# The last convolution of a four-layer network: other engines for its evictions, stores and loads

## The chip, the cores and the metric

The kernel runs on one core of a Trainium2 chip. The core has five engines that run side by side: TensorE (PE in the profile; its weight loads have a row of their own, PEld), VectorE (DVE), ScalarE (ACT), GpSimd (POOL) and SyncE (SP), the last of which does no arithmetic. SyncE, ScalarE and GpSimd can issue transfers between the chip's memory and SBUF; the profile shows the issuing as SPq, ACTq and POOLq. Matrix products land in PSUM, which has eight banks of 512 float32 columns on each of 128 partitions. The metric is the device time of one execution in microseconds; less is better.

## The reference

The input x is (8 images, 16 channels, 256, 256) in float32. Four layers follow each other, and each adds a convolution-like function of the group-normalised x to x: capsule routing, a spline convolution, patch attention, and last a 3x3 convolution. Only the last one matters here:

```
x = x + conv(_gn(x), L3_conv_weight)     # 16 -> 16 channels, 3x3
```

The reference writes this convolution with Fourier transforms, and the border wraps around: row -1 is row 255. The corner rows and columns of the transform's diagonal pick all nine taps. The group norm has eight groups of two channels each, over one image.

## The kernel before, in words

The four layers run one after another, each layer's result going through a scratch tensor in the chip's memory. `layer3` begins when the last rows of the third layer's result are on their way to the scratch tensors `x3_0` to `x3_7`, one for each image.

**Layout.** An image lies in SBUF as 128 partitions: eight row residues times sixteen channels. A partition holds 32 rows of 258 columns, the two edge columns wrapped, and a 33rd row for the wrap at the bottom. The weights `ws` contain the reciprocal deviation of the image's group norm and the identity that adds x itself; `weights` makes them for the next image with one VectorE instruction. What the mean contributes is a bias for each output row, `stat[b][1]`.

**Steps and pairs.** An image is four steps (`s` = 0 to 3), handled as two pairs: steps 0 and 1, then steps 2 and 3. Sixteen pairs make the stage. For a step, `products` is called twice, with `q` = 0 and 1; each call issues 48 products of a 32x32 weight block with 32x512 data, three column shifts times four banks `j` times four column blocks `c`. The profile shows each product as two records, so that one call is 96 records and a pair 384. The order in a pair, on TensorE, is q=0 of the first step, q=0 of the second, q=1 of the first, q=1 of the second.

**PSUM.** The products of a step go to a tile `p3` of four banks (named `p` in the profile). The pool has two of them, so that a pair fills all of PSUM, and the next pair's first step reuses the first tile, its second step the second tile. After q=0 of a step, ScalarE copies a few elements of it to `seen`; q=1 of that step waits for this.

**Eviction and stores.** `finish` (L1532 to L1547) takes a step from PSUM to the SBUF tile `y3` (named `y` in the profile, three buffers): ScalarE evicts the tile's first two banks and adds the bias, then VectorE the other two. Eight stores of 128 KB follow, four issued by SyncE and four by ScalarE itself; a store at the image's lower edge is split in two.

**Loads.** The first image is mostly in SBUF already (`first`); the rest of it (`x3r`, `x3e`) is loaded at the stage's start. `fetch` loads a whole image, in four pieces of 1032 KB and one small one, into one of three buffers, from SyncE. Images 1 and 2 are fetched at the start; image n+2 is fetched after the first pair of image n. SyncE issues these between its stores.

**Order.** Inside `tc.manual_schedule()` each engine runs its instructions in the order in which the code issues them. The last image's group norm isn't known when the stage starts; its steps (`todo`, from `stats3_steps`) are laid in after the first six pairs, each with a small product into a tile `p3` of the same pool, and VectorE or ScalarE work.

The waits between engines are made by the framework from the tiles that an instruction reads and writes.

Of the kernel before, what the change touches and what calls it, by code (L numbers as in the profile page):

```python
# [10 lines left out]
F32 = mybir.dt.float32  # L11
AF = mybir.ActivationFunctionType
ALU = mybir.AluOpType
AX = mybir.AxisListType
PSUM = bass.MemoryType.PSUM
DRAM = bass.MemoryType.DRAM

B, C, H, W = 8, 16, 256, 256
P = 128
WP = W + 2  # L20
# [258 lines left out]
class _Net:  # L279
# [1195 lines left out]
    def layer3(self, images=range(B)):  # L1475

        nc, tc = self.nc, self.tc
        with ExitStack() as st:
            io = st.enter_context(tc.tile_pool(name="l3_io", bufs=2))
            psum = st.enter_context(tc.tile_pool(name="l3_ps", bufs=2, space=PSUM))
            stat = dict.fromkeys(images, self.bc3)

            def bank():
                t = []

                def get():  # L1490
                    if not t:
                        t.append(psum.tile([P, 4, 512], F32, name="p3"))
                    return t[0][:, 0]

                return get

            def fetch(b):
                xs = io.tile([P, 33, WP], F32, name="x3s", bufs=3)
                self.fetch3(b, 0, 33, xs)
                return lambda k, g: xs[32 * k : 32 * k + 32, g : g + 2]  # L1500

            def weights(b):
                ws = io.tile([P, 3, 2, 32], F32, name="ws3")
                nc.vector.scalar_tensor_tensor(
                    ws.rearrange("p d t m -> p (d t m)"),
                    self.w3.rearrange("p d t m -> p (d t m)"),
                    stat[b][0][:, 1, b : b + 1],
                    self.k["ident3"],
                    ALU.mult,
                    ALU.add,  # L1510
                )
                return ws

            def products(s, q, ws, xs, ps):

                for dw in range(3):
                    for j in range(4):
                        k = (j + q) % 4
                        for c in range(4):
                            g = 8 * s + 2 * c + (j + q) // 4  # L1520
                            nc.tensor.matmul(  # L1521
                                ps[32 * c : 32 * c + 32, j].rearrange("p (g w) -> p g w", w=W),
                                ws[32 * k : 32 * k + 32, dw, q],
                                xs(k, g)[:, :, dw : dw + W],
                                start=q == 0 and dw == 0,
                                stop=q == 1 and dw == 2,
                                skip_group_check=True,
                            )

            def finish(b, s, ps):  # L1530

                y = io.tile([P, 2, 4, W], F32, name="y3", bufs=3)  # L1532
                bias = stat[b][1][:, b : b + 1]
                src = ps.rearrange("p j (g w) -> p g j w", w=W)
                nc.scalar.activation(y[:, :, 0:2], src[:, :, 0:2], AF.Identity, bias=bias)
                nc.vector.tensor_scalar(y[:, :, 2:4], src[:, :, 2:4], bias, None, ALU.add)
                for c in range(4):
                    for ro in range(2):
                        row = 64 * s + 16 * c + 1 + ro
                        n = 8 if row + 14 < H else 7  # L1540
                        yc = y[32 * c : 32 * c + 32].rearrange("(o r) g j w -> r o (g j) w", r=2)[ro]
                        for first, m, at in ((0, n, row),) if n == 8 else ((0, 7, row), (7, 1, 0)):
                            to = self.out[b, 0, at]
                            (nc.scalar if c % 2 else nc.sync).dma_start(
                                out=bass.AP(tensor=to.tensor, offset=to.offset, ap=[[H * W, C], [2 * W, m], [1, W]]),
                                in_=yc[:, first : first + m],
                            )  # L1547

            images = list(images)
            rest = io.tile([P, 9, WP], F32, name="x3r", bufs=1)  # L1550
            self.fetch3(images[0], 24, 9, rest)
            edge = io.tile([P, 3, WP], F32, name="x3e", bufs=1)
            nc.sync.dma_start(
                out=edge, in_=self.x3[images[0]].rearrange("r c h k w -> (r c) (h k) w")[:, 23:26]
            )

            def first(k, g):
                part = slice(32 * k, 32 * k + 32)
                if g + 2 <= 24:
                    return self.x3s[part, g : g + 2]  # L1560
                return edge[part, g - 23 : g - 21] if g == 23 else rest[part, g - 24 : g - 22]

            seen = io.tile([P, 4], F32, name="seen", bufs=1)
            xs = {images[0]: first}
            ws = weights(images[0])

            stat[images[-1]], todo = self.stats3_steps(self.small, "g3b", bank)
            with tc.manual_schedule():
                for b in images[1:3]:
                    xs[b] = fetch(b)  # L1570
                for n, b in enumerate(images):
                    for s in (0, 2):
                        ps = [psum.tile([P, 4, 512], F32, name="p3") for _ in range(2)]
                        for q in range(2):
                            for k in range(2):
                                products(s + k, q, ws, xs[b], ps[k])
                                if q:
                                    finish(b, s + k, ps[k])
                                else:
                                    nc.scalar.copy(seen, ps[k][:, :, 0])  # L1580
                        if todo:
                            todo.pop(0)[2]()
                        while todo and todo[0][0] != "PE":
                            todo.pop(0)[2]()
                        if s == 0 and n + 1 < len(images):
                            if n and n + 2 < len(images):
                                xs[images[n + 2]] = fetch(images[n + 2])
                            ws_after = weights(images[n + 1])
                    if n + 1 < len(images):
                        ws = ws_after  # L1590
# [69 lines left out]
```

## Time and profile before

| What | us |
|---|---|
| Median of three runs (6789.7 to 6796.36) | 6793.12 |
| The profiled execution's own time | 6794.16 |
| Its span in the profile | 6792.4 |
| First product of the last convolution (from the span's start) | 6452.8 |
| End of its last product | 6779.2 |
| VectorE evictions, 128x1024, each | 1.284 |
| ScalarE evictions, 128x1024, each | 1.113 |

The profile's times count from the start of the span. A line of the timeline gives the start, the duration, the engine, the source line, the operation, output and inputs, and in square brackets how long the engine had been idle and what ended that. In the view of waits, a line names who waited, for whom, the total in microseconds, how often, and the longest. In the table of stretches, each engine has its busy time and number of instructions, and then come the granted TensorE clock (1.00 is full speed), the busy share of the 16 DMA engines, and GB/s. Line numbers are those of the code above: L1521 a product, L1535 ScalarE's eviction, L1536 VectorE's, L1544 a store, L1469 and L1473 an image's load, L1504 the weights, L1580 the copy to `seen`.

### The profile page before, as it was taken

The numbers are of one execution on the slowest core, as the hardware profiler recorded it, in microseconds if no ns is written. First come the engines' busy times: TensorE is split into PE (matmuls) and PEld (weight loads), VectorE is DVE, ScalarE is ACT, GpSimd is POOL, SyncE is SP. The second block draws the span as 40 slices with busy tenths as digits, with TensorE's granted clock in tenths as the row PEclk, the third lists the DMA queues.
The fourth block names the chain that finished last, engine by engine and source line by source line (L and its number), as shares of the span: only waits on it lengthen the run. The fifth ranks groups of instructions, "written<-read, shape, count | busy, mean of one in ns | idle before, by whom it ended". The sixth has DMA issues, their size and how long they took to land. (4 is left out here: it accounts for less than half of the span.)

```text
span 6792.4 us, 111546 instructions
## 1 busy us (share of the span) xinstructions
PE 6136.1 (90%) x46024; PEld 2773.5 (41%) x46024; DVE 5395.3 (79%) x6342; ACT 2738.6 (40%) x3898; POOL 3219.0 (47%) x2077
## 2 busy tenths in 40 slices
PE   3899889899898999899886999999999999999977
PEld 1333333333333333333332444444444566666643
DVE  5799999999999999999997999999999433333311
ACT  1333333333333333333331888888888222112211
POOL 0566666666666666666666344444443211111100
PEclk9999999999999999999997999999999999999988
DMA  6233333333333333333331555555556433433266
GB/s 257 60 89 92 95 87 93 92 89 87 87 87 87 87 92 95 91 89 93 92 88 57 188 175 176 175 175 175 176 177 182 136 80 95 102 92 81 61 205 182
DMA packets 394912, 801.07 MB, mean 118 GB/s; under 512 B 57506, under 2 KB 222626, under 8 KB 355106
## 3 DMA queue, kind: packets, MB, share of 16 engines
q1 hardware_dynamic: 342050, 743.33, 37.3%
q10 hardware_dynamic: 52352, 50.61, 2.5%
q8 instruction: 361, 5.91, 0.4%
q14 instruction: 149, 1.22, 0.1%
HBM read 583.07 MB, written 210.77 MB: 117 GB/s over the span
## 5 line engine op out<-in xcount | busy, mean ns | idle before, releaser
L745 POOL TENSOR_TENSOR dd<-dd 128x1024 f32<-128x1024 f32 x512 | 1213.8, 2371 | 616.8 <-DVE dd L736 596.7
L1001 PE MATMUL ps<-bases,tw 128*32 128x512 f32 (+1 forms) x13824 | 1361.3, 546 | 16.4 <-POOL bases L970 6.6
L736 DVE SCALAR_TENSOR_TENSOR dd<-rb,v 128x1024 f32<-128x1024 f32 (+1 forms) x1024 | 1066.9, 1083 | 96.8 <-PE rb L725 89.8
L970 POOL TENSOR_TENSOR bases<-e,a 128x1024 f32<-128x1024 f32 (+1 forms) x264 | 621.7, 2377 | 928.9 <-DVE e L968 928.6
L624 DVE TENSOR_TENSOR pr<-v,fb 128x2048 f32<-128x2048 f32 (+1 forms) x512 | 1011.5, 2017 | 24.3 <-PE pl L634 12.9
L518 PE MATMUL cv<-kt,w 128*128 128x512 f32 x2048 | 1001.3, 611 | 28.7 <-DVE dd L736 21.5
L527 ACT COPY v<-cv 128x1024 f32<-128x1024 f32 x512 | 517.1, 1010 | 1152.0 <-PE cv L522 1152.0
L1001 PEld LDWEIGHTS ps<-bases,tw 128*32 128x32 f32 x13824 | 597.3, 109 | 801.8 <-issue 483.8
L745 POOL TENSOR_TENSOR s<-s,dd 128x512 f32<-128x512 f32 x512 | 670.8, 1310 | 35.0
L725 PE MATMUL rb<-rs,ct_fold 32*128 32x512 f32 x3584 | 608.0, 648 | 71.3 <-ACT rs L707 67.9
L745 POOL TENSOR_TENSOR s<-v,dd 128x512 f32<-128x512 f32 x256 | 330.2, 1290 | 663.2 <-DVE dd L736 663.2
L634 PE MATMUL pl<-pr,ct_fold 128*32 128x512 f32 x3584 | 533.7, 608 | 120.7 <-DVE pr L624 120.7
L522 PE MATMUL cv<-kt,w 64*128 64x512 f32 x2048 | 578.3, 641 | 0.0
L518 PEld LDWEIGHTS cv<-kt,w 128*128 128x128 f32 x2048 | 354.9, 191 | 525.5 <-issue 300.5
L1415 PE MATMUL pqk<-w_qk,t 128*128 128x512 f32 x1024 | 484.2, 595 | 4.6 <-POOL t L1409 4.6
L1426 ACT ACTIVATE vt<-pv,w_b2v 128x128 f32<-128x128 f32 x512 | 146.2, 368 | 843.9 <-PE pv L1422 843.9
L1447 DVE TENSOR_TENSOR y<-po,res 128x512 f32<-128x512 f32 x128 | 88.5, 691 | 487.3 <-PE po L1442 487.3
L978 DVE SCALAR_TENSOR_TENSOR bases<-xr,xm,bases 128x1024 f32<-128x1024 f32 (+1 forms) x264 | 447.9, 1735 | 0.3 <-POOL bases L970 0.3
L1409 POOL TENSOR_TENSOR t<-t,emb 128x512 f32<-128x512 f32 x128 | 162.2, 1268 | 512.2 <-DVE t L1405 501.9
L955 ACT ACTIVATE sq<-a 128x1024 f32<-128x1024 f32 (+1 forms) x264 | 263.8, 999 | 230.0 <-DVE a L947 229.3
L725 PEld LDWEIGHTS rb<-rs,ct_fold 32*128 32x128 f32 x3584 | 172.8, 185 | 414.9 <-issue 219.3
L937 ACT ACTIVATE d<-xr,bd,sd 128x1024 f32<-128x1024 f32 (+1 forms) x264 | 319.1, 1209 | 15.7 <-DMA xr<-x1p 15.7
(260 smaller groups left out, 8386.8 us busy)
## 6 DMA issues: line engine op xcount, KB each, us to landing
kt<-d SPq DMA_DIRECT2D x256, 516.0 KB
xr<-x1p SPq DMA_DIRECT2D x120, 1024.0 KB
d<-dn ACTq DMA_DIRECT2D x64, 516.0 KB
x<-y SPq DMA_DIRECT2D x128, 258.0 KB
xs<-in_x_dram SPq DMA_DIRECT2D x16, 2048.0 KB
xs<-in_x_dram SPq DMA_DIRECT2D x64, 512.0 KB
res<-in_x_dram SPq DMA_DIRECT2D x64, 512.0 KB
x<-s SPq DMA_DIRECT2D x128, 256.0 KB
```

The costliest lines, as they stand in the source:

```text
L518: nc.tensor.matmul(ps()[:, n], w[:, 0, j, :], t[:, a : a + 2, 0:W], start=True, stop=False)
L522: nc.tensor.matmul(ps()[:, n], w[at, 1, j, :], t[at, a : a + 2, 2 - n : 2 - n + W], start=False, stop=True)
L527: nc.scalar.copy(v[h]()[:, 4 * g : 4 * g + 4, j * W : j * W + W], ps().rearrange("p n (a w) -> p (n a) w", w=W),)
L624: nc.vector.tensor_tensor(pr()[:, :n].rearrange("p n (r w) -> p n r w", w=W), v[h]()[:, 4 * g : 4 * g + n].rearrange("p n (r w) -> p n r w ...
L634: nc.tensor.matmul(pl()[at : at + 32], sel[:, g, h, :], pr()[:, t, :], start=h == 0 and g == 0, stop=h == 1 and (g == 1 or t == 3),)
L725: nc.tensor.matmul(r()[:, n], spread[at, g, h, :], rs()[at], start=True, stop=True)
L736: nc.vector.scalar_tensor_tensor(dd()[:, :n], r()[:, :n], 1.0 / B, v[h]()[:, a : a + n], ALU.subtract, ALU.mult)
L745: op("POOL", us, lambda: nc.gpsimd.tensor_tensor(out[0](), a[0](), b[0](), ALU.add), a[1] + b[1], out[1])
L970: nc.gpsimd.tensor_tensor(ring[n % 3][:, 0, p : p + m, 1 : 1 + W], rows(e), rows(a), ALU.subtract)
L978: nc.vector.scalar_tensor_tensor(r, rows(part[1]), xm[:, b : b + 1], v, ALU.is_gt, ALU.mult)
L1001: nc.tensor.matmul(out if k is None else out[:, k], lhs, rhs, start=start, stop=stop, skip_group_check=True)
L1415: nc.tensor.matmul(ps, t[:, n, k * P : (k + 1) * P], wqk[:, n, :], start=n == 0, stop=n == 1)
```

## The change

Four things change in `layer3`; the arithmetic stays.

- A step's PSUM tile of four banks becomes two tiles of two banks, from a pool of four. The small products of `todo` take one such tile.
- In `finish`, ScalarE evicts both halves of an even step, and VectorE both halves of an odd step. The copy to `seen` is divided in the same way, one for each half and with a tile of its own for each engine. `y3` has five buffers.
- SyncE issues all stores.
- GpSimd's queue loads half images of 17 or 16 rows (and the small wrapped piece), in one transfer each, into five buffers. Five halves are fetched at the start; from the fourth pair on, a pair begins by fetching the half that is needed four pairs later.

```
-            psum = st.enter_context(tc.tile_pool(name="l3_ps", bufs=2, space=PSUM))
+            psum = st.enter_context(tc.tile_pool(name="l3_ps", bufs=4, space=PSUM))
...
-            def fetch(b):
-                xs = io.tile([P, 33, WP], F32, name="x3s", bufs=3)
-                self.fetch3(b, 0, 33, xs)
-                return lambda k, g: xs[32 * k : 32 * k + 32, g : g + 2]
+            def fetch(n):
+                xs = io.tile([P, 17, WP], F32, name="x3s", bufs=5)
+                rows = self.x3[images[n // 2]].rearrange("r c h k w -> (r c) (h k) w")
+                if n % 2:
+                    nc.gpsimd.dma_start(out=xs[:, :16], in_=rows[:, 16:])
+                    nc.gpsimd.dma_start(out=xs[:32, 16], in_=rows[:32, 0])
+                else:
+                    nc.gpsimd.dma_start(out=xs, in_=rows[:, :17])
+                return lambda k, g: xs[32 * k : 32 * k + 32, g - n % 2 * 16 : g - n % 2 * 16 + 2]
...
-                y = io.tile([P, 2, 4, W], F32, name="y3", bufs=3)
+                y = io.tile([P, 2, 4, W], F32, name="y3", bufs=5)
                 bias = stat[b][1][:, b : b + 1]
-                src = ps.rearrange("p j (g w) -> p g j w", w=W)
-                nc.scalar.activation(y[:, :, 0:2], src[:, :, 0:2], AF.Identity, bias=bias)
-                nc.vector.tensor_scalar(y[:, :, 2:4], src[:, :, 2:4], bias, None, ALU.add)
+                for k in range(2):
+                    src = ps[k].rearrange("p j (g w) -> p g j w", w=W)
+                    to = y[:, :, 2 * k : 2 * k + 2]
+                    if s % 2:
+                        nc.vector.tensor_scalar(to, src, bias, None, ALU.add)
+                    else:
+                        nc.scalar.activation(to, src, AF.Identity, bias=bias)
...
-                            (nc.scalar if c % 2 else nc.sync).dma_start(
+                            nc.sync.dma_start(
...
-                for b in images[1:3]:
-                    xs[b] = fetch(b)
+                for n in range(2, min(7, halves)):
+                    xs[n] = fetch(n)
                 for n, b in enumerate(images):
                     for s in (0, 2):
-                        ps = [psum.tile([P, 4, 512], F32, name="p3") for _ in range(2)]
+                        i = 2 * n + s // 2
+                        if 7 <= i + 4 < halves:
+                            xs[i + 4] = fetch(i + 4)
+                        ps = [[psum.tile([P, 2, 512], F32, name="p3") for _ in range(2)] for _ in range(2)]
...
-                                    nc.scalar.copy(seen, ps[k][:, :, 0])
+                                    for h in range(2):
+                                        (nc.vector.tensor_copy if k else nc.scalar.copy)(
+                                            seen[k][:, h], ps[k][h][:, :, 0]
+                                        )
...
-                            if n and n + 2 < len(images):
-                                xs[images[n + 2]] = fetch(images[n + 2])
```

More of the change, by code (lines that the diff above doesn't have):

```diff
@@ L1491, in get @@
                     if not t:
-                        t.append(psum.tile([P, 4, 512], F32, name="p3"))
+                        t.append(psum.tile([P, 2, 512], F32, name="p3"))
                     return t[0][:, 0]
                 return get
-            def fetch(b):
-                xs = io.tile([P, 33, WP], F32, name="x3s", bufs=3)
-                self.fetch3(b, 0, 33, xs)
-                return lambda k, g: xs[32 * k : 32 * k + 32, g : g + 2]
+            def fetch(n):
[7 more added lines that the diff above has]
+                return lambda k, g: xs[32 * k : 32 * k + 32, g - n % 2 * 16 : g - n % 2 * 16 + 2]
             def weights(b):
@@ L1521, in products @@
                             nc.tensor.matmul(
-                                ps[32 * c : 32 * c + 32, j].rearrange("p (g w) -> p g w", w=W),
+                                ps[j // 2][32 * c : 32 * c + 32, j % 2].rearrange("p (g w) -> p g w", w=W),
                                 ws[32 * k : 32 * k + 32, dw, q],
@@ L1561, in first @@
                 return edge[part, g - 23 : g - 21] if g == 23 else rest[part, g - 24 : g - 22]
-            seen = io.tile([P, 4], F32, name="seen", bufs=1)
-            xs = {images[0]: first}
+            seen = [io.tile([P, 2, 2], F32, name=f"seen{k}", bufs=1) for k in range(2)]
+            halves = 2 * len(images)
+            xs = {0: first, 1: first}
             ws = weights(images[0])
@@ L1568, in layer3 @@
             with tc.manual_schedule():
-                for b in images[1:3]:
-                    xs[b] = fetch(b)
+                for n in range(2, min(7, halves)):
+                    xs[n] = fetch(n)
                 for n, b in enumerate(images):
                     for s in (0, 2):
-                        ps = [psum.tile([P, 4, 512], F32, name="p3") for _ in range(2)]
+                        i = 2 * n + s // 2
+                        if 7 <= i + 4 < halves:
+                            xs[i + 4] = fetch(i + 4)
+                        ps = [[psum.tile([P, 2, 512], F32, name="p3") for _ in range(2)] for _ in range(2)]
                         for q in range(2):
                             for k in range(2):
-                                products(s + k, q, ws, xs[b], ps[k])
+                                products(s + k, q, ws, xs[i], ps[k])
                                 if q:
```

## The prediction

> **What bounds the kernel now.** Only the last stage is touched, so I cut everything to it: from 6452.8 us, the first product, to the end. The page's busy shares are averages over four layers and say nothing here. The view of waits, for 6452 to 6793, comes first:
>
> ```profile
> DVE y L1536 <- ACT y L1535: 234.3, 23, 15.6
> ACT y L1535 <- DMA out_dram<-y: 109.9, 16, 13.7
> ...
> PE p L1521 <- DVE y L1536: 55.8, 13, 11.3
> ...
> PE p L1521 <- issue: 15.2, 9, 2.3
> ...
> PE p L1521 <- DVE g3b_m L1175: 4.9, 1, 4.9
> ...
> PE p L1521 <- DVE g3b_v L1194: 3.5, 1, 3.5
> ```
>
> VectorE waits for ScalarE, ScalarE for stores, TensorE for VectorE: a ring in which TensorE is last. The timeline of 6735 to 6793, after the last load, shows its plainest turn:
>
> ```profile
> 6735.14 3.41 PE L1521 MATMUL p<-x3s,ws 32*32 32x512 f32 x96 [2.16 <-DVE y L1536]
> ...
> 6738.92 9.76 PE L1521 MATMUL p<-x3s,ws 32*32 32x512 f32 x288 [0.37 <-ACT seen L1580]
> ...
> 6744.82 3.47 ACTq L1544 DMA_DIRECT2D out_dram<-y  x4
> ...
> 6748.50 1.11 ACT L1535 ACTIVATE y<-p,g3a_bias 128x1024 f32<-128x1024 f32 x1 [5.02 <-DMA out_dram<-y]
> 6749.65 1.28 DVE L1536 TENSOR_SCALAR y<-p,g3a_bias 128x1024 f32<-128x1024 f32 x1 [4.85 <-DMA out_dram<-y]
> ...
> 6750.98 14.48 PE L1521 MATMUL p<-x3s,ws 32*32 32x512 f32 x384 [2.31 <-DVE y L1536]
> ```
>
> The 288 records are q=1 of both steps and, unblocked, q=0 of the next pair's first step. The odd step's q=1 ends at about 6745.4 (6738.92 plus two thirds of 9.76), but ScalarE is issuing the even step's four stores until 6748.29 and evicts only at 6748.50; VectorE follows, and TensorE, which needs the second tile, stands still for 2.31 us. The stores hadn't been late: ScalarE's hands were full. The clock falls as well, as the table by single microseconds shows around this stop (columns: stretch, its length, busy time and count of PE, PEld, DVE, ACT, POOL, then granted clock, DMA share, GB/s):
>
> ```profile
> 6743.00:6744.00 1.00, 1.00 (x50) 0.77 (x34) 0.49 (x1) 0.47 (x1) 0.00 (x0) 1.00 0.06 16
> ...
> 6747.00:6748.00 1.00, 1.00 (x54) 0.59 (x31) 0.00 (x0) 0.00 (x0) 0.00 (x0) 1.00 0.94 214
> ...
> 6751.00:6752.00 1.00, 1.00 (x32) 0.43 (x33) 0.00 (x0) 0.00 (x0) 0.00 (x0) 0.50 0.03 9
> ```
>
> In image stretches with loads the stop is longer. The chain of 6590 to 6680 has it:
>
> ```profile
> 6616.72 10.12 DMA x3s<-x
> 6626.83 0.02 issue
> 6626.85 6.35 DMA out_dram<-y
> 6633.20 0.17 issue
> 6633.37 1.12 ACT y L1535
> 6634.49 0.03 issue
> 6634.52 1.29 DVE y L1536
> ```
>
> SyncE's stores stood behind an image's load, y wasn't free, and TensorE waited 7.3 us, to 6635.85.
>
> [...] ScalarE pays 0.88 us an issue (median), and a step's megabyte moves in about 5 us (6785.8 to 6790.4) though two queues carry it. [...]
>
> **The change, part by part.** *What TensorE needs.* 96 + 288 records took 3.41 + 9.76 = 13.17 us at full clock; sixteen pairs are 210.7 us. It now takes 6779.2 - 6452.8 = 326.4 us, 20.4 a pair. Of the 115.7 us between, the waits account for 55.8 + 15.2 + 4.9 + 3.5 + 1.5 (on seen) = 80.9[...].
>
> *Eviction by step parity, two-bank tiles.* An even step costs ScalarE 2 x 1.113 = 2.23 us, an odd one VectorE 2 x 1.284 = 2.57, against 2.4 in series now. The first tile's reuse comes 3.3 us of q=1 later (a quarter of 13.17), the second's 3.3 us of q=0 later. Both fit without a stop, so the cover is 0.7 to 1.1 us. Were it gone, a pair would lose what is missing, and nothing more. ScalarE's copies (0.162 us, two) and VectorE's two have 3.3 us. Cost on the path: nothing.
>
> *Stores to SyncE.* ScalarE loses 136 issues of 0.88 us, 120 us, and with them its lateness: the 55.8 us of waits, the 1.5 on seen and nearly all of the 34.8 go. SyncE gets 264 issues. At its present 0.60 us they are 158 us, 9.9 a pair of 13.2. A step's eight take 4.8 us, about the time of their transfer. Under a load an issue has taken up to 1.485; that end is a rival. Queued behind a waiting store there is only the next store, and for these nobody waits but y.
>
> *y from three buffers to five.* A step's buffer is needed 5 x 6.6 = 33 us later; eviction, issue and transfer take 2.6 + 4.8 + about 4 = 11.4. The slack of 21 us covers lateness from loads; when it is spent, eviction waits and then TensorE.
>
> *Loads on GpSimd's queue.* GpSimd does nothing in this stage (0.00 in every stretch), and SyncE's stores no longer stand in line behind a load. A half is 17 x 1032 B x 128 = 2.25 MB (16 rows: 2.11, and 33 KB), 3% more for an image than now. This kernel's trace has no transfer from GpSimd's queue. From above: SyncE's large loads move 400 to 420 GB/s when alone (6470 to 6474), 5.4 us a half. [...] From below: cut into small packets they would move like the stores, 215 GB/s (0.94 share, above), 10.4 us a half. I take 415, since each partition's rows are contiguous. The five first halves with the rest of image 0 are 12.5 MB, 30 us; the half for pair 2 lands first and is needed near 6491. Each later one has four pairs, over 50 us. So a load isn't waited for. [...]
>
> [...] The stops on issue that TensorE now has: 1.52 + 1.45 for image 3's load, 2.09 + 1.73 for image 4's (later loads fall into stops that go). I take the larger, 3.8 us for 4.26 MB, times the seven images that are loaded: 27 us. Ends: 15 (today's sum) and 40 (every stop 3 us).
>
> *Statistics of the last image.* Six products in the tile pool now make TensorE wait 4.9 and 3.5 us and more. With quarter tiles the next pair's third bank belongs to an odd step's first half: 1.28 us of VectorE less the 0.6 us of the two banks ahead[...], and the products' own 0.7. Six times 1.9 = 11 us.
>
> *Start and end.* Half clock over the first 4 us: 2. The end now takes 13.2 us after the last product, with ScalarE 2.9 us late. Then: SyncE is still issuing the even step's stores until 3.9 us after the last product, the last nine take 5.5, and from the last issue's end to the end there are 3.7 (6788.7 to 6792.4): 13.1. No gain.
>
> *Sum.* 210.7 + 27 + 11 + 2 = 251 from 6452.8: 6703.5; plus 13.1 is a span of 6717. The profiled execution's own time lies 1.8 above its span, and 1.0 above the median shown: 6718. The DMA engines: stores 33.6 MB at 215 are 156 us, loads 32.2 MB at 415 are 78, together 234, less than 251 though not by much; I add 4 us for it: **6722**, a gain of 71 us or 1.0%.
>
> **The rivals.** *Stores starved.* If GpSimd's loads move at 215 GB/s, a pair with a load needs 9.8 + 10.4 = 20.2 us of DMA against 15.1 of TensorE [...], 5 us more in nine pairs, 46 in all; y's slack hides the first 20 and the opening burst of 58 us instead of 30 uses that up: 6722 + 46 = 6768. For it speaks that a DMA share of 0.94 at 214 GB/s already appears with stores alone; against it the 400 to 420 GB/s of large packets.
>
> *SyncE the bound, slower than before.* All stores hang on one engine that waits for each issue. At t us each, the stage takes 264 t plus 16 before the first (6452.8 to 6469.3) and 4 after the last; that equals today's 339.6 at t = 1.21. If the average comes to 1.4, near the largest seen under a load, it is 264 x 1.4 + 20 = 390, and the kernel takes 6843. Against it: the median of 0.60 with the other queue busy too, and loads fill only a third of the stage.
>
> [...] 27 falls to 5, time 6700. Today's opening, 1.22 and 2.02 us lost under continuous load, speaks against it.
>
> *The wait only moves.* If the transfers and not their issuing set the pace, y would stop ScalarE as it does now, about 6790. Against it: the DMA engines do nothing between 6744 and 6746 and again from 6757 to 6762.
>
> **How the numbers follow.** Forecast 0.60, its own range 6700 to 6745; stores starved 0.20; [...] SyncE the bound 0.06; the wait only moves 0.03. From 6694 to 6772 the first three fit, and less than 2 in 10 is left out. A change under 0.2%, 13.6 us, is about what a measurement of this kernel can't tell from none. Faster: the first three, 0.91; same 0.03; slower 0.06.
>
> **What would show it.** Right: the last product ends near 6703; ScalarE's wait for stores and VectorE's for ScalarE are gone; TensorE's waits are led by "issue", below 40 us; the clock is 1.00 in all stretches after 6510; sixteen pairs take about 13.2 us without a load and 15 with one. SyncE's stores keep a median near 0.6 us. Wrong: evictions that wait for stores (stores starved, or SyncE), TensorE waiting for a load of x3s, or a pair without a load well above 13.2 us, which would mean that I misread what holds TensorE.

## The result and the profile after

The changed kernel takes 6722.12 us (median of four runs, 6718.79 to 6726.08) against 6793.58 (6789.70 to 6796.36) for the kernel before: a ratio of 0.9895, with a 95% interval of 0.9878 to 0.9913. The forecast was 6722, in a range of 6694 to 6772. The profiled execution took 6718.79 us, with a span of 6716.9.

The stage, cut as in the prediction (us; "tail" is from the end of the last product to the end of the span):

| | before | predicted | after |
|---|---|---|---|
| first product | 6452.8 | 6452.8 | 6447.4 |
| last product ends | 6779.2 | 6703.5 | 6697.9 |
| first product to last | 326.4 | 250.7 | 250.5 |
| tail | 13.2 | 13.1 | 19.1 |
| span | 6792.4 | 6717 | 6716.9 |

The total is right, but not all of its parts are. The view of waits of the changed kernel, for 6440 to 6720 (columns: engine and line, what it waited for, us in total, times, longest), shows what became of the ring:

```profile
ACT y L1545 <- DMA out_dram<-y: 41.6, 6, 8.8
DVE y L1543 <- DMA out_dram<-y: 35.2, 6, 6.1
PE p L1526 <- issue: 22.3, 16, 2.5
PE p L1526 <- DVE ws L1509: 5.9, 1, 5.9
```

TensorE's waits for VectorE's eviction (55.8 us before) are no longer there, nor those for the copies to `seen` and for the statistics. It is left with "issue" (it waited for nothing that the profile shows) and with the wait before its first product. The evictions still wait for stores, but nothing comes of it for TensorE, as the timeline of 6630 to 6717 shows (columns: start, length, what, and in brackets the idle time before it and what ended that):

```profile
6628.74 85.52 SPq L1553 DMA_DIRECT2D out_dram<-y  x105
6638.17 59.72 PE L1526 MATMUL p<-x3s,ws 32*32 32x512 f32 x1732 [2.51 <-issue]
...
6656.33 2.12 ACT L1545 ACTIVATE y<-p,g3a_bias 128x1024 f32<-128x1024 f32 x2 [5.84 <-DMA out_dram<-y]
6659.17 2.48 DVE L1543 TENSOR_SCALAR y<-p,g3a_bias 128x1024 f32<-128x1024 f32 x2 [5.56 <-DMA out_dram<-y]
```

The products run in one piece from 6638.17 to the end, while the two evictions shown are let go by a store's end, not by a product's. A row of issues is counted from its first issue to its last, waits between them included. SyncE's row of 105 stores holds one wait of 4.64 us, from 6634.65 to 6639.29; after it SyncE issues to the end with no pause above 0.33 us, and hardly anything separates it from the pace of TensorE. Its row in the list of stores (shortest, median and longest issue in ns, then the first and the last start), and its longest entry in the view of waits from 6485 on:

```profile
L1553 SPq DMA_DIRECT2D out_dram<-y x264: 554/601/2179, 6464.1 to 6713.6; - x132
```

```profile
SPq L1553 <- DMA out_dram<-y: 38.0, 10, 4.8
```

The median of 601 ns is the 0.60 us of the forecast, but 39 of the 264 took over 0.7 us, and all of them together 187.4 us: a mean of 0.71. On top of that come the waits of the entry above, 38.0 us in ten, for stores that SyncE had issued earlier and that had not landed. In each of the nine later loads SyncE's longest wait of this kind was 2.7 to 4.8 us, and it ended within 0.5 us of the load's landing (the load issued at 6629.63 landed at 6639.09, SyncE's wait ended at 6639.29).

The table of stretches (columns as in the prediction) has the clock after two stops, and the tail:

```profile
6509.00:6510.00 1.00, 0.92 (x33) 0.41 (x33) 0.00 (x0) 0.00 (x0) 0.00 (x0) 1.00 0.27 92
...
6526.00:6527.00 1.00, 1.00 (x33) 0.27 (x2) 0.00 (x0) 0.00 (x0) 0.00 (x0) 0.50 0.70 162
...
6610.00:6620.00 10.00, 9.22 (x270) 6.31 (x257) 2.64 (x3) 1.50 (x4) 0.55 (x1) 1.00 0.98 296
...
6704.00:6714.00 10.00, 0.00 (x0) 0.00 (x0) 0.00 (x0) 0.00 (x0) 0.00 (x0) 0.50 0.88 201
```

After a stop of 1.53 us (it ended at 6509.08) the clock is 1.00; after one of 1.98 us (at 6525.22) it is 0.50. In a_y3, below, it is 1.00 after a stop of 3.10 us, so the length of a stop alone didn't decide it in these runs. In the tail nothing runs but stores, at 201 GB/s.

### The profile page after: what moved, and what is told of

Same layout as the page of the kernel before. It is cut to its first block, busy times and chain, and to the rows that moved or that the text cites. A ratio compares the mean times of both kernels' runs of the same rounds, so it can differ in the third digit from the quotient of the medians.

```text
span 6716.9 us, 111531 instructions
## 1 busy us (share of the span) xinstructions
PE 6114.0 (91%) x46024; PEld 2774.9 (41%) x46024; DVE 5400.4 (80%) x6374; ACT 2737.3 (41%) x3898; POOL 3230.2 (48%) x2098
## 5 line engine op out<-in xcount | busy, mean ns | idle before, releaser
L624 DVE TENSOR_TENSOR pr<-v,fb 128x2048 f32<-128x2048 f32 (+1 forms) x512 | 1011.6, 2017 | 24.1 <-PE pl L634 12.7
L937 ACT ACTIVATE d<-xr,bd,sd 128x1024 f32<-128x1024 f32 (+1 forms) x264 | 319.0, 1208 | 15.8 <-DMA xr<-x1p 15.8
```

The costliest lines, as they stand in the source:

```text
L624: nc.vector.tensor_tensor(pr()[:, :n].rearrange("p n (r w) -> p n r w", w=W), v[h]()[:, 4 * g : 4 * g + n].rearrange("p n (r w) -> p n r w ...
```

## The experiments

The theory was the prediction's: ScalarE's store issues made its eviction late, and taking them away is the gain; what remains is TensorE's time, stopped by "issue" while loads run. The rivals were that one of the other parts (the eviction by parity, the loads on GpSimd's queue, five buffers of y) gives the gain, and that SyncE now sets the end. All ratios are to the kernel before, run on the same chip (6793.1, 6793.06 and 6793.75 us in the three groups of runs). In the first three experiments one part of the change is made alone in the kernel before; the others change the changed kernel.

| run | median us | ratio (95%) | products us | tail us |
|---|---|---|---|---|
| changed kernel | 6722.12 | 0.9895 (0.9878 to 0.9913) | 250.5 | 19.1 |
| b_stores | 6739.29 | 0.9924 (0.9909 to 0.9939) | 267.8 | 16.1 |
| b_evict | 6763.75 | 0.9957 (0.9943 to 0.9972) | 296.2 | 11.7 |
| b_loads | 6807.67 | 1.0020 (1.0012 to 1.0027) | 342.6 | 13.4 |
| a_split | 6803.66 | 1.0017 (1.0009 to 1.0025) | 336.3 | 11.8 |
| a_noload | 6691.14 | 0.9850 (0.9833 to 0.9866) | 220.0 | 20.0 |
| a_small | 6713.59 | 0.9884 (0.9870 to 0.9899) | 248.1 | 13.8 |
| a_y3 | 6729.69 | 0.9907 (0.9892 to 0.9922) | 259.0 | 15.6 |
| a_sync_loads | 6726.60 | 0.9902 (0.9888 to 0.9917) | 247.8 | 28.2 |
| a_even | 6726.14 | 0.9901 (0.9887 to 0.9916) | 259.9 | 11.0 |
| a_halves | 6726.68 | 0.9901 (0.9887 to 0.9916) | 250.4 | 26.1 |
| best_late | 6720.89 | 0.9894 (0.9879 to 0.9909) | 251.4 | 14.1 |
| best_all | 6714.92 | 0.9883 (0.9867 to 0.9900) | 250.4 | 11.1 |

"Products" is from the start of the first product to the end of the last. It and the tail are of the profiled execution. The diffs below are cut to the lines that matter.

**b_stores: only the stores go to SyncE.**

```diff
-                            (nc.scalar if c % 2 else nc.sync).dma_start(
+                            nc.sync.dma_start(
```

> The kernel before with one edit: SyncE issues all stores; loads, eviction and buffers stay. Theory A (ScalarE's store issues make the odd step's eviction late, and TensorE stops for it): a pair without a load falls from 16.7 us to near 13.2, since eviction in series takes 2.4 us and has 3.3; pairs with a load keep their stop, because the stores still stand behind the load on SyncE's queue and y has three buffers: about 6750. Rival B (the loads in the stores' queue are what costs): hardly a gain or a loss, 6780 to 6810, since SyncE now has every store behind its loads.

Measured: 6739.29 us, 53.8 less than before, three quarters of the whole gain from one line. The waits of TensorE for an eviction fall from 55.8 us to:

```profile
PE p L1521 <- DVE y L1536: 20.5, 8, 5.6
...
PE p L1521 <- issue: 10.5, 9, 1.8
```

What is left of them goes with the other parts of the change.

**b_evict: only the eviction by parity, from two-bank tiles, with `seen` in two halves.** ScalarE still issues half of the stores.

```diff
-                        ps = [psum.tile([P, 4, 512], F32, name="p3") for _ in range(2)]
+                        ps = [[psum.tile([P, 2, 512], F32, name="p3") for _ in range(2)] for _ in range(2)]
...
+                    if s % 2:
+                        nc.vector.tensor_scalar(to, src, bias, None, ALU.add)
+                    else:
+                        nc.scalar.activation(to, src, AF.Identity, bias=bias)
```

> The kernel before with one edit: two-bank PSUM tiles, even steps evicted by ScalarE, odd ones by VectorE, the copies to seen divided alike; stores still half from ScalarE, loads from SyncE, three y buffers. Theory A: the odd step's eviction no longer stands behind ScalarE's issues, so that a pair without a load falls to near 13.2 us here too, with the stop at loads kept: about 6750. Rival B (loads in the stores' queue): about 6785.

Measured: 6763.75 us, 29.4 less. Now VectorE evicts a whole odd step and no longer waits for ScalarE to begin. ScalarE is as late as ever, and it is its copies to `seen` that TensorE waits for:

```profile
ACT seen L1585 <- DMA out_dram<-y: 145.2, 12, 17.0
...
PE p L1521 <- ACT seen L1585: 32.9, 14, 7.9
```

**b_loads: only the loads, as half images on GpSimd's queue, with five buffers for them.**

```diff
-                self.fetch3(b, 0, 33, xs)
+                    nc.gpsimd.dma_start(out=xs, in_=rows[:, :17])
...
+                        if 7 <= i + 4 < halves:
+                            xs[i + 4] = fetch(i + 4)
```

> The kernel before with one edit: half images loaded from GpSimd's queue into five buffers; stores, eviction and y as before. Theory A: the 2.3 us stop and the half clock after it stay in every pair, some 16.7 us a pair, and only the long stops at loads go: about 6765. Rival B: most of the gain, 6730.

Measured: 6807.67 us, 14.6 more than before; both readings had expected a gain. This part alone makes the kernel slower. A turn of its timeline:

```profile
6609.99 8.44 ACTq L1549 DMA_DIRECT2D out_dram<-y  x4
6618.48 0.35 ACT L1589 COPY seen<-p 128x4 f32<-128x4 f32 x2 [9.84 <-DMA out_dram<-y]
6618.69 12.08 PE L1526 MATMUL p<-x3s,ws 32*32 32x512 f32 x288 [3.67 <-ACT seen L1589]
```

ScalarE takes 8.44 us from the first of four issues to the end of the last (3.47 in the prediction's turn without a load). The issues themselves are 3.2 us of it. From 6610.58 to 6615.73 ScalarE waits for an earlier store of its own to land; it lands at 6615.71, just after the load beside it (6615.53). The copies to `seen` come after these issues, and TensorE stops for 3.67 us. With a half image on its own queue in most pairs, ScalarE meets a load in each of these; before, an image came once in two pairs.

**a_split: the changed kernel, but ScalarE issues every second store again.**

```diff
-                            nc.sync.dma_start(
+                            (nc.scalar if c % 2 else nc.sync).dma_start(
```

> The changed kernel with one edit undone: ScalarE again issues every second store. [...] the time stays within 6 us of 6722, and only the end after the last product shortens from 19 us to about 14. If SyncE's 264 stores in a row set it (they run without a pause from 6464 to 6714 us in the profile of the changed kernel), the time falls by 5 us or more. If ScalarE's issuing as such costs TensorE time, it rises by 30 us: but the odd step's eviction isn't behind it any more.

Measured: 6803.66 us, and not within 6 us of 6722, as it should have been if TensorE's own time set the end (the prediction's reading). All of the gain is lost with this one line, and 10 us more. Waits and a turn of the timeline:

```profile
ACT seen L1594 <- DMA out_dram<-y: 175.6, 12, 20.9
...
PE p L1526 <- ACT seen L1594: 69.5, 15, 9.5
```

```profile
6650.78 15.79 ACTq L1553 DMA_DIRECT2D out_dram<-y  x8
...
6666.62 0.22 ACT L1594 COPY seen<-p 128x2 f32<-128x2 f32 x2 [15.86 <-DMA out_dram<-y]
6666.83 15.55 PE L1526 MATMUL p<-x3s,ws 32*32 32x512 f32 x381 [6.24 <-ACT seen L1594]
```

Eight issues and the waits between them hold ScalarE for 15.79 us, longer than a pair of steps should last. The list of stores, for these eight, shows that issuing is the smaller part:

```profile
L1553 ACTq DMA_DIRECT2D out_dram<-y x8: 584/736/1183, 6650.8 to 6666.0; - x8
```

Together the eight issues take 6.4 us. The longest wait between them, 7.85 us up to 6664.68, is for a store that ScalarE had issued at 6652.34 and that landed at 6664.65; a load issued at 6652.24 landed at 6664.25. TensorE stops for 6.24 us and then runs the pair in 15.55. After the last load the stops are short: TensorE waits 3.9 us for the copies to `seen` from 6724 to 6790, against 57.8 from 6485 to 6715. A pair still takes 15.5 us there (three pairs from 6733.14 to 6779.61), so that issuing alone costs time as well. So the stores' engine is the cause of the gain: alone it gives 54 us, and on top of the other parts 82. The three single results add up to -68.6 us, close to the -71.5 of the change, but this is no proof that they are independent: without the stores' move, the other parts together (a_split, +10.6) are 25 us worse than the sum of the two (-29.4 + 14.6).

**a_noload: the changed kernel without its nine later loads.** The nine half images that are fetched inside the loop are not loaded, and the products use a half that was loaded earlier.

```diff
-                            xs[i + 4] = fetch(i + 4)
+                            xs[i + 4] = xs[2 + i % 2]
```

> The changed kernel without its nine later loads: from the fourth pair's fetch on, the halves of image 1 are read again in place of those that would have been loaded, so that the loads of images 3 (second half) to 7 are left out. [...] the last product comes 15 to 20 us earlier, and the stops on issue after 6490 vanish. The stores then have the DMA engines to themselves; if SyncE's stores set the end only because loads held them up, the end after the last product falls from 19 to about 14 us: about 6698 in all. If SyncE's issuing by itself sets the end (264 in a row at 0.65 us are 172 us of 250), no stop remains and the time is the same 6698[...].

Measured: 6691.14 us, products in 220.0 us instead of 250.5. The loads cost TensorE 30.5 us, more than the 15 to 20 that I had expected from the prediction's estimate (27 us for seven images, 1.9 a half). The wait on "issue", from the view of waits, and then the last ten pairs, from the timeline:

```profile
PE p L1526 <- issue: 4.5, 4, 1.8
```

```profile
6543.06 127.23 PE L1526 MATMUL p<-x3s,ws 32*32 32x512 f32 x3832
```

Ten pairs in 127.23 us are 12.72 us each: that is a pair with nothing in its way. (The changed kernel runs at 12.8 us a pair in its last unbroken stretch, at a clock of 1.00 from 6650 to 6690.) The tail stays at 20.0 us and the mean issue at 0.74 us, though no load runs after the opening: SyncE's issues are not long because of the loads alone. Its waits for earlier stores do go: 11.0 us in the whole stage, against 48.8 in the changed kernel.

**a_small: the loads in pieces of four rows** (4128 B for each partition instead of 17.5 KB).

```diff
-                    nc.gpsimd.dma_start(out=xs, in_=rows[:, :17])
+                    for k in range(0, 17, 4):
+                        nc.gpsimd.dma_start(out=xs[:, k : min(k + 4, 17)], in_=rows[:, k : min(k + 4, 17)])
...
```

> The changed kernel with each half image loaded in four or five transfers of four rows (4128 B a partition in place of 17.5 KB), same queue, same buffers. [...] the stops on issue fall from 22 us to about 12, and 6712. If the amount of data alone counts, 6722. [...] SyncE's backlog at the end should shrink by some microseconds too.

Measured: 6713.59 us, the lowest median of the versions that load their whole input, 8.5 less than the changed kernel's; the intervals of the two ratios overlap, so that the gain is likely and not shown. The waits on "issue" are a little shorter, 18.0 us against 22.3 and not the 12 that I had estimated, with a longest of 1.7 us instead of 2.5; that it is the size of a transfer that sets them isn't shown.

```profile
PE p L1528 <- issue: 18.0, 17, 1.7
```

Products take 2.4 us less than in the changed kernel, and the tail 5.3 less.

**a_y3: y has three buffers again.**

```diff
-                y = io.tile([P, 2, 4, W], F32, name="y3", bufs=5)
+                y = io.tile([P, 2, 4, W], F32, name="y3", bufs=3)
```

> The changed kernel with three y buffers in place of five. The prediction gave five buffers a slack of 21 us for late stores; with three the next use comes 13.2 us earlier and the slack is 8. In the profile of the changed kernel stores lie behind by more than that during loads (evictions wait 77 us for stores even with five), so TensorE should stop at most pairs with a load: 9 times some 3 us, about 6750. If five buffers aren't needed, 6722.

Measured: 6729.69 us, 7.6 more; the intervals overlap, but the products of the profiled execution take 8.5 us more. What the two buffers cover is seen in the waits: an eviction that has to wait for a store now stops TensorE.

```profile
PE p L1526 <- DVE y L1543: 10.3, 3, 8.8
```

**a_sync_loads: the half images are loaded through SyncE's queue**, between its stores.

```diff
...
-                    nc.gpsimd.dma_start(out=xs, in_=rows[:, :17])
+                    nc.sync.dma_start(out=xs, in_=rows[:, :17])
```

> The changed kernel with the half-image loads issued by SyncE in place of GpSimd, at the same places in the order. If the stores' queue matters (stores stand behind a load on the same engine), SyncE's chain, which has no pause as it is, grows by 21 issues and by the time that stores wait for loads, and the time rises to 6745 or more. If the same DMA engines and the same bytes are all that counts, 6722. The kernel before with only the stores moved to SyncE, which had loads on SyncE and three y buffers, took 6739.

Measured: 6726.60 us, 4.5 more, with overlapping intervals. The products are as fast as in the changed kernel (247.8 us); only the tail is longer, 28.2 us. SyncE waits 41.5 us for loads in this version, and all that comes of it lies at the end. In the changed kernel it waits no less, 48.8 us, for its own stores to land: a queue for the loads does not free the stores from them. Once ScalarE issues nothing, which queue carries the loads is worth a few microseconds at most.

**a_even: ScalarE issues every second store of even steps only**, a quarter of all, after its own evictions.

```diff
-                            nc.sync.dma_start(
+                            (nc.scalar if c % 2 and s % 2 == 0 else nc.sync).dma_start(
```

> The changed kernel, but ScalarE issues every second store of the even steps, which it evicts itself; it never waits for VectorE, and has four issues in a pair where the run with every second store of all steps had eight and took 6804. If ScalarE's copies to seen behind its own issues are what costs, four issues (3.5 us) fit into the 9.9 us before the copy holds TensorE up, SyncE has 12 stores a pair in place of 16, and the end after the last product falls from 19 us towards 13: 6716. If any issue on ScalarE costs, because it waits for transfers that stand behind loads, half the loss comes back: 6760.

Measured: 6726.14 us, 4.0 more, with overlapping intervals. The tail falls to 11.0 us, so it was SyncE that made it long. But the products take 259.9 us:

```profile
ACT seen L1594 <- DMA out_dram<-y: 24.6, 3, 14.2
...
PE p L1526 <- ACT seen L1594: 5.7, 2, 5.5
```

Four issues in a pair were enough to make ScalarE late while a load was under way. In the longer of the two stops, ScalarE waited 7.75 us, up to 6545.50, before its last issue, and a load landed at 6544.69. What the tail gains, the products lose.

**a_halves: the old division, ScalarE one half and VectorE the other of each step**, with all else as changed.

```diff
-                    if s % 2:
+                    if k:
```

> The changed kernel with the old division of the eviction: in every step ScalarE takes the first half and VectorE the second, from the two-bank tiles; stores, loads and buffers as changed. If the division by step is worth nothing once ScalarE issues no stores (the prediction: both fit in the 3.3 us), 6722. If the halves follow each other as before and the copies come later for it, 5 to 10 us more. It can't gain by more than 1 us a step at the end.

Measured: 6726.68 us, 4.6 more, with overlapping intervals; the products take 250.4 us, as before this edit. Who evicts which step makes no difference to TensorE as soon as ScalarE issues no stores. The tail is longer, 26.1 us, with a mean issue of 0.74 us; why, these runs don't show.

**best_late and best_all: a_small, with GpSimd issuing some of the stores**, every second one in the last two images, or those of the fourth column block in all of them.

```diff
-                            nc.sync.dma_start(
+                            (nc.gpsimd if c % 2 and b in images[6:] else nc.sync).dma_start(
```

```diff
-                            nc.sync.dma_start(
+                            (nc.gpsimd if c == 3 else nc.sync).dma_start(
```

> The changed kernel with loads in transfers of four rows (6714 when alone), and in the last two images, when no loads are left, GpSimd issues every second store. If SyncE's issuing (0.71 us and a gap of 0.05, sixteen and a half times a pair, 12.5 us of 13.2) makes the end late, the end after the last product falls from about 16 to 12 us: 6708 to 6710. If the transfers themselves do, 6714.

> The changed kernel with loads in transfers of four rows, and GpSimd issues a quarter of the stores (the fourth column block) in all pairs. SyncE then has 12 stores a pair, 9.3 us of 13.2. If SyncE is the limit, the backlog doesn't arise and the time is 6705; if stores behind loads on GpSimd's queue are late for the five y buffers, 6720 to 6740, and the view of waits shows evictions waiting for stores longer than the 110 us of the run with small transfers alone.

Measured: 6720.89 and 6714.92 us, both higher than expected. In best_late the tail is 14.1 us, no shorter than a_small's 13.8. In best_all it is 11.1 us, and SyncE now waits 87.3 us for evictions, so it has time to spare:

```profile
SPq L1555 <- ACT y L1547: 87.3, 16, 14.9
```

Products take 250.4 us against a_small's 248.1, and the total is the same. Relieving SyncE shortens the tail by a few microseconds and no more: TensorE's own time is right behind. Of the versions tried, a_small is the one to keep, since it is the simpler of the two with the lowest medians.

## Why the prediction was right, point by point

The changed kernel's products can be cut with two of its own numbers and a_noload's 12.72 us a pair. Image 0's two pairs end where the third begins, at 6485.32: 37.9 us, 12.5 over two clean pairs. The 14 pairs after that take 212.6, which is 34.5 over 14 clean ones. In a_noload the four pairs with statistics take 54.4 us (6488.69 to 6543.06), 3.5 over four clean pairs; so 31.0 of the 34.5 belong to the nine loads, in agreement with the 30.5 by which the two kernels' products differ. Two of the six small products of the statistics lie in image 0's pairs and are counted with the opening.

| term | predicted | measured |
|---|---|---|
| sixteen pairs | 16 x 13.17 = 210.7 | 16 x 12.72 = 203.5 |
| stops on "issue", opening and its clock | 27 + 2 | 12.5 + 31.0 = 43.5 |
| statistics | 11 | 3.5 (four of the six) |
| sum, first product to last | 250.7 | 250.5 |
| tail | 13.1 | 19.1 |
| start of the stage | 6452.8 | 6447.4 |
| added for the DMA engines | 4 | none |

*What bounds the kernel.* Right in that ScalarE's storing was the cause. The stops went when the stores left ScalarE, and they came back with them, now through the copies to `seen`; b_stores and a_split show this from both sides. But the prediction held only the time of the issues against ScalarE, 120 us in all. In the kernel before they do come to 112.3 us; in a_split's turn, beside a load on another queue, the waits for earlier stores to land were the larger part, over 9 us against 6.4 of issues.

*What TensorE needs.* Oversized by 0.45 us a pair, 7 us in all. Its 3.41 + 9.76 us are two rows with a stop between them. A product's record lasts 0.59 us (median, in the changed kernel) and overlaps the ones after it, so that each row's end has a full record that an unbroken run would have once: 13.17 less 0.59 is 12.58. That accounts for the excess, and a little more. What makes up the 34.8 us that the waits leave of the 115.7 isn't shown: in the kernel before the clock was 0.50 after some stops and 1.00 after others (figures in the last section).

*Eviction by step parity: nothing on the path.* Right for the change as a whole (a_halves). It would have been wrong as a statement about this part alone: in the kernel before it is worth 29 us, most likely because it frees VectorE from waiting for a late ScalarE. The same edit costs or gives according to what else has been done.

*Stores to SyncE.* The direction was right, the price of an issue was too low: 0.71 us in the mean (187.4 over 264). The trace before could have told: SyncE's 128 issues had a median of 0.60 there too, but a mean of 0.74. A pair has 16.5 issues; at 0.71 plus the 0.04 that usually lie between one and the next, that is 12.4 us of SyncE, not 9.9, against TensorE's 12.7. The issuing alone leaves SyncE almost no slack, and the waits for landing come on top of it, 48.8 us over the stage, for which the prediction had no term. The evictions' waits for stores (41.6 and 35.2 us) are their mark; the prediction had named such waits as a sign that it was wrong, and they cost TensorE nothing only because five buffers cover them. The rival "SyncE the bound" was nearer than its chance said, though its own deciding point, 1.21 us, was far off.

*y with five buffers.* Right that they cover, and they are used: with three, TensorE waits 10.3 us for evictions.

*Loads on GpSimd's queue.* "SyncE's stores no longer stand in line behind a load" was named as a gain. They don't stand in its queue, but they still wait for it: SyncE's longest waits end within 0.5 us of the loads' landing. The other queue is worth about 4.5 us, within the noise (a_sync_loads), and alone the part is a loss of 14.6 us. The rate was wrong as well: a half image lands 10.0 us after its issue in the median, not 5.4, as the list of `x3s` has it:

```profile
DMA to landing us min/median/max: 8.8/10.0/30.5
```

This is the lower bound of 10.4 us on which "stores starved" rests. That rival failed all the same, because it gave a load and its pair's stores 215 GB/s in all. Together they move more: 296 GB/s in the stretch of 6610 to 6620 above, against 201 for stores alone.

*Stops on "issue".* Undersized: 43.5 us with the opening and its half clock (0.50 from 6447 to 6450), beyond the upper end of 40 for the stops and the 2 for the clock. The 22.3 us of waits on "issue" are only half of it. Of the rest, the timeline of the products shows where some lies:

```profile
6509.08 5.35 PE L1526 MATMUL p<-x3s,ws 32*32 32x512 f32 x140 [1.53 <-issue]
...
6525.22 6.96 PE L1526 MATMUL p<-x3s,ws 32*32 32x512 f32 x142 [1.98 <-issue]
```

At 12.72 us a pair, 142 records are 4.70 us; after the longer stop they took 6.96, with the clock at 0.50. The prediction counted the waits on issue and not the half clock behind some of them, and expected a clock of 1.00 in every stretch after 6510. The rival in which the 27 us fall to 5, with a chance of 0.11, is out. What TensorE stands still for in these stops no run shows; there are more of them when there are loads: 22.3 us with the nine loads, 4.5 without.

*Statistics.* Oversized. In the changed kernel TensorE doesn't wait for them at all; they cost 3.5 us over four pairs, 0.9 each and not 1.9, which was an estimate.

*Start and end.* The tail was undersized by 6 us, for the reason given under SyncE: when the last product ends at 6697.9, SyncE still issues for 16 us, 25 stores, more than three steps' worth. In a_even and best_all, where SyncE has less to do, the tail is 11 us. The start of the stage moved by 5.4 us with nothing changed ahead of it; over all runs it lies between 6446.7 and 6456.5.

So the right total came about by cancellation, which is luck: 14.5 us too little for the stops on "issue" and the opening against 7.2 and 7.5 too much for pairs and statistics; 6.0 too little for the tail against 5.4 at the start. The 4 us added for the DMA engines correspond to nothing in the traces; that the median lies 3.3 us above the profiled execution hides it. What the prediction can claim is which engine's work had to go and the rough size of the gain, not the last digits.

*Not settled.* Why an issue on SyncE takes 0.71 to 0.74 us in the mean with a median of 0.60, even without loads. It isn't that every issue slows down beside busy DMA engines: in best_all GpSimd issued 72 of the same stores in 0.51 to 0.57 us each, while SyncE's went up to 1.92:

```profile
L1555 SPq DMA_DIRECT2D out_dram<-y x192: 577/606/1916, 6467.5 to 6709.5; - x192
L1555 POOL DMA_DIRECT2D out_dram<-y x72: 508/532/568, 6481.1 to 6705.6; - x72
```

What it is in the queues of SyncE and ScalarE, no run tells. Nor does any run show why some stores land only when a load beside them has landed.

## What to carry to other kernels

An engine that evicts should not issue the stores of what it evicts if its next short operation is needed by another engine: beside a load, ScalarE waited 7.85 us between two of its issues for an earlier store to land (a_split), and everything behind it in ScalarE's order waited too. Before moving loads to a queue of their own, take compute engines out of the store path; in the other order the same edit cost 14.6 us here (b_loads). When one engine issues all stores, take the mean of its issue times and not the median (0.71 and 0.60 us here), add its waits, and set the sum beside the time of one loop of the engine that you want to be the bound. And a row of a timeline that merges several issues is not their busy time: look inside it before you call an engine busy.

## What the runs showed of the hardware

- Eight store issues and the waits between them held ScalarE for 15.8 us beside a load on GpSimd's queue (a_split): 6.4 us of issuing, and most of the rest waiting for earlier stores; the longest wait, 7.85 us, was for one that landed 0.4 us after the load. On GpSimd itself the issue of a 2.2 MB load took 0.53 us (median, changed kernel).
- In six microseconds of the kernel before (6474 to 6480), with loads on SyncE's queue, that queue moved 2.01 MB and ScalarE's, with its stores, 0.33 MB.
- The clock after a stop of TensorE was 0.50 after 1.98 us (changed kernel, to 6525.22), 1.64 us (a_even, to 6602.94) and 2.31 us (kernel before, to 6750.98). It was 1.00 after 1.53 us (changed kernel, to 6509.08), 2.24 us (kernel before, to 6694.36) and 3.10 us (a_y3, to 6579.44; its row and the stretch after it are below). The length of the stop alone didn't decide.
- Nine loads of 2.2 MB, none of which TensorE waited for, made its products 30.5 us longer. With loads in pieces of four rows the longest stop was 1.7 us instead of 2.5.

```profile
6579.44 10.21 PE L1526 MATMUL p<-x3s,ws 32*32 32x512 f32 x290 [3.10 <-issue]
...
6580.00:6581.00 1.00, 1.00 (x47) 0.53 (x25) 0.16 (x1) 0.00 (x0) 0.00 (x0) 1.00 0.23 80
```
